# Layer 3's scans: where the additions over states run, who copies the exponents, and how many buffers they have

## The chip, the cores and the metric

The kernel runs on one core of a Trainium2 chip. A core has five engines that each work through their own list of instructions in order: PE (TensorE, matmul), DVE (VectorE), ACT (ScalarE), POOL (GpSimd) and SP (SyncE), which here mostly issues DMAs. They wait for each other by semaphores. The metric is the time of the whole kernel in microseconds on the device, the median over runs.

## The reference

Four layers are applied to x of shape (4, 96, 56, 56), each as x + layer(group norm of x): attention, a selective scan over eight directions, a windowed top-k aggregation, and a second kind of scan over four directions. Only the last one's scan is touched. For each direction k, batch b, channel d (192) and position t (3136), with 16 states n:

```python
dA  = dlt[..., None] * A_log[None, :, :, None, :]
phi = jnp.exp(-jnp.cumsum(dA, axis=3))
dbx = dlt[..., None] * jnp.swapaxes(b, 2, 3)[:, :, None] * xs[..., None]
h   = phi * jnp.cumsum(dbx / (phi + 1e-12), axis=3)
y   = jnp.einsum('bkdln,bknl->bkdl', h, c) + Ds[None, :, :, None]
```

So phi is the exponential of a running sum, the input is divided by phi (plus a tiny number), summed up along t, and multiplied by phi again; the last line adds up the 16 states with weights c.

## The kernel before, in words

`cumulative` does this. The positions are cut into chunks of 93 and a chunk into three blocks of 31. Two directions (one forward, one backward) go side by side, so a chunk has six blocks, taken in pairs; there are 34 chunks for each of two pairs of directions: 68 chunks, 408 blocks. In a block, partition 32b+t is batch b and position t (31 positions and one row for the carry), and the free dimension has 6 groups of channels x 16 states x 32 channels = 3072 elements.

What is done for one block, with the lines of the profile:

- `zhalf(st, h)`, twice: PE multiplies the running sums of delta by A for eight of the states (L1297) into a PSUM tile `z` that has one buffer. ScalarE copies it (L1305, 1536 elements) into its half of the tile `phi`, which at first holds exponents. The first half also allocates `phi`, from a pool with five buffers.
- `inverse(st)`: ScalarE's sigmoid of phi gives 1/(exp + tiny) into `w` (L1313, three buffers). `phis(st)`: ScalarE turns phi into exponentials in place (L1321). Each has its table load (1283 ns).
- `weights(st)`: PE brings delta times u into a PSUM tile `misc` (L1329); GpSimd builds the matrix `m` from C, the triangle and B (L1336 to L1338, three buffers).
- `into_sum(st)`: VectorE multiplies w by that tile in place (L1345); then SP loads the carry of this direction, 48 KB, from the DRAM tensor `l3cr` into four rows of w (L1346).
- `sums(st, q)`, q = 0 to 3: PE multiplies m by w for four states each (L1357) into a PSUM tile `q` with two buffers.
- `times(st, q)`: VectorE multiplies phi by that in place, 768 elements (L1366).
- `carry(st)`: SP stores four rows of phi to `l3cr` (L1370). The block after next, which is of the same direction, loads them in its L1346.
- `out(st)`: the sum over the 16 states. VectorE adds the halves of phi into a tile `t` (L1376, 1536 elements) and the halves of that (L1377, 768); GpSimd adds 384 elements (L1378) and 192 into `y` (L1380, two buffers); SP stores y with four DMAs (L1388).

`prepare` makes a chunk's inputs, the chunk before being at work. It is a generator; `tick` runs it to its next `yield`, twice for each block. Its pieces are loads of u, small matmuls with copies on ScalarE, two softplus (the "wide" step, L1186 and L1191 to L1193, which use the tile z), loads of C (L1199), du on GpSimd (L1228), and for each direction VectorE's L1233, a scan of 752 elements (L1241) and L1243.

The order is written out by hand. `in_order` chains the instructions of each engine, SP's DMAs among them, in the order in which the program calls them; nothing is rescheduled. The loop at the end of `cumulative` works on the pair `now`, prepares the pair `nxt` and starts the exponents of `third`. For one block st, with `coming_up` the next: inverse or phis of a later block, weights(coming_up), times 0 and 1, sums 2 and 3, zhalf(third, 0), inverse or phis of another, into_sum(coming_up), times 2 and 3, carry(st), tick, zhalf(third, 1), sums 0 and 1 of coming_up, tick, out(st). If the tick was the wide one, zhalf(third, 1) comes after the two sums.

Of the kernel before, what the change touches and what calls it, by code (L numbers as in the profile page):

```python
# [9 lines left out]
F32 = mybir.dt.float32  # L10
AF = mybir.ActivationFunctionType
ALU = mybir.AluOpType
# [9 lines left out]
DI, NS, R = 192, 16, 6  # L22
# [9 lines left out]
def view(ap, offset, dims):  # L32

    return bass.AP(ap.tensor, ap.offset + offset, [ap.ap[0], *dims])
# [35 lines left out]
class Net:  # L70
# [1027 lines left out]
    def cumulative(self, us, dram):  # L1098


        nc, tc = self.nc, self.tc
# [6 lines left out]
        with in_order(tc), ExitStack() as cx:  # L1108
# [179 lines left out]
            def zhalf(st, h):  # L1288
                s, i = st["s"], st["i"]
                lo = TW - TB * (i + 1) if s["rev"] else TB * i  # L1290
                st["lo"] = lo
                z = psz.tile([128, 3, 2, 8, 32], F32, name="z")
                for dh in range(2):
                    for b in range(B):
                        for p in range(3):
                            ps_ = slice(32 * p, 32 * p + 32)
                            nc.tensor.matmul(  # L1297
                                z[32 * b : 32 * b + 32, p, dh].rearrange("p n d -> p (n d)"),
                                s["s"][ps_, dh, b, lo : lo + 32],
                                st["ad"][ps_, dh, 8 * h : 8 * h + 8, :].rearrange("p n d -> p (n d)"),  # L1300
                                start=True, stop=True,
                            )
                if h == 0:
                    st["phi"] = big.tile([128, 3, 2, NS, 32], F32, name="phi", bufs=5)
                nc.scalar.copy(  # L1305
                    st["phi"][:, :, :, 8 * h : 8 * h + 8, :].rearrange("p a b n d -> p a b (n d)"),
                    z.rearrange("p a b n d -> p a b (n d)"),
                )
# [63 lines left out]
            def out(st):  # L1372
                s, i, lo, k = st["s"], st["i"], st["lo"], st["k"]
                phi = st["phi"].rearrange("p a b n d -> p (a b) (n d)")
                t = p2.tile([128, 6, 8 * 32], F32, name="t", bufs=1)
                nc.vector.tensor_tensor(t, phi[:, :, 0:256], phi[:, :, 256:512], ALU.add)  # L1376
                nc.vector.tensor_tensor(t[:, :, 0:128], t[:, :, 0:128], t[:, :, 128:256], ALU.add)  # L1377
                nc.gpsimd.tensor_tensor(t[:, :, 0:64], t[:, :, 0:64], t[:, :, 64:128], ALU.add)  # L1378
                y = p2.tile([128, DI], F32, name="y")
                nc.gpsimd.tensor_tensor(  # L1380
                    view(y, 0, [[32, 3], [96, 2], [1, 32]]),
                    view(t, 0, [[512, 3], [256, 2], [1, 32]]), view(t, 32, [[512, 3], [256, 2], [1, 32]]),
                    ALU.add,
                )
                a, e = max(lo, s["off"]), min(lo + TB, s["off"] + s["tv"])
                at = s["t0"] + a - s["off"]
                for b in range(B):
                    nc.sync.dma_start(  # L1388
                        ys[k][b, at : at + e - a, :], y[32 * b + a - lo : 32 * b + e - lo, :]
                    )  # L1390
# [5 lines left out]
            def draw():  # L1396
                return [next(todo, None) for _ in range(2)]

            now, nxt = draw(), draw()
            for st in (*now, *nxt):  # L1400
                zhalf(st, 0)
# [9 lines left out]
            while now[0] is not None:  # L1411
                third = draw()
                for i, st in enumerate(now):
                    coming_up = (now[1], nxt[0])[i]
                    what = (inverse, phis)[i]
                    if nxt[0] is not None:
                        what(nxt[0])
                    if coming_up is not None:
                        weights(coming_up)
                    times(st, 0)  # L1420
                    times(st, 1)
                    sums(st, 2)
                    sums(st, 3)
                    if third[i] is not None:
                        zhalf(third[i], 0)
                    if nxt[1] is not None:
                        what(nxt[1])
                    if coming_up is not None:
                        into_sum(coming_up)
                    times(st, 2)  # L1430
                    times(st, 3)
                    carry(st)
                    wide = tick()[1]
                    if third[i] is not None and not wide:
                        zhalf(third[i], 1)
                    if coming_up is not None:
                        sums(coming_up, 0)
                        sums(coming_up, 1)
                    if third[i] is not None and wide:
                        zhalf(third[i], 1)  # L1440
                    tick()
                    out(st)
                now, nxt = nxt, third
        return ys

    def layer3(self, xin, xout, dram):
# [284 lines left out]
```

## Time and profile before

| | us |
|---|---|
| three runs, median | 16579.15 |
| lowest and highest | 16575.54, 16581.78 |
| the profiled execution | 16544.92 |
| its span | 16543.1 |
| first to last L1366 (layer 3's scans) | 10927.2 to 15715.9 |
| mean granted clock of TensorE | 0.911 |

Busy over the whole span: PE 13366.7 us (81%), DVE 13918.8 (84%), ACT 12240.4 (74%), POOL 7665.0 (46%). These are averages over four layers with different limits; for this change the stretch in the table's fifth row counts. A row of the groups reads: line, engine, operation, output<-inputs, shapes, how often, then busy time and mean duration in ns, then the idle time of that engine just ahead of it and what ended it. A row of the timeline is start, length, engine, line, operation, and in brackets the idle time ahead of it and its releaser. "SPq" is SP's queue of DMA issues, and its length is the time for issuing, not for the transfer.

### The profile page before, as it was taken

What the parts mean: (1) busy time and instruction counts of PE and PEld (TensorE: products, weight loads), DVE (VectorE), ACT (ScalarE), POOL (GpSimd) and SP (SyncE); (2) the same over time, 40 slices, a digit from 0 to 9 for tenths busy, and PEclk for the clock granted to TensorE, in tenths of its full rate; (3) what the DMA queues carried; (4) which work ended last, traced back from release to release, by engine and by line L of the source; (5) the groups of instructions that cost most, each with busy time, mean ns of one, the idle gap of its engine ahead of it and who ended that gap; (6) DMA issues with size and microseconds to landing.
All of it is one profiled execution on the core that took longest, in us unless ns stands there. A gap on an engine that the chain in (4) does not pass through costs nothing.

```text
span 16543.1 us, 501276 instructions
## 1 busy us (share of the span) xinstructions
PE 13366.7 (81%) x221976; PEld 8983.6 (54%) x221976; DVE 13918.8 (84%) x15345; ACT 12240.4 (74%) x15452; POOL 7665.0 (46%) x3968
## 2 busy tenths in 40 slices
PE   8999977777777777777776678778888888888866
PEld 4333325666666666666665445446666656666533
DVE  7666549999999999999998777768888888888866
ACT  0465449999999999999996244468888888888822
POOL 0000028888888888888885000023333333333300
PEclk6899889999999999999998588889999999999977
DMA  0000034334444434344445800122212222221122
GB/s 15 1 1 1 16 137 97 91 92 95 105 105 103 103 91 96 92 96 102 103 105 139 194 10 10 43 71 51 50 47 50 50 50 51 51 50 47 43 66 66
DMA packets 821402, 1152.50 MB, mean 70 GB/s; under 512 B 309360, under 2 KB 728720, under 8 KB 807456
## 3 DMA queue, kind: packets, MB, share of 16 engines
q1 hardware_dynamic: 759872, 1055.38, 26.3%
q10 hardware_dynamic: 53984, 45.77, 1.2%
q8 instruction: 1745, 28.59, 0.8%
q0 software_dynamic: 5376, 19.27, 0.4%
q14 instruction: 425, 3.48, 0.1%
HBM read 842.93 MB, written 277.18 MB: 68 GB/s over the span
## 4 chain that ended last, share of the span: by engine, by line
PE 32%; DVE 28%; ACT 19%; issue 15%; DMA 5%; SPq 1%; POOL 1%; DVEq 0%; ACTq 0%; POOLq 0%
DVE q L638 17%; PE q L1357 7%; ACT ht L663 5%; PE s L233 4%; ACT e L626 3%; PE d L417 3%; ACT phi L1305 3%; DVE w L1345 3%; PE z L1297 2%; PE acc L251 2%; PE m L196 2%; ACT w L1313 2%; PE t L561 2%; PE y L675 2%; DVE phi L1366 2%
## 5 line engine op out<-in xcount | busy, mean ns | idle before, releaser
L618 POOL TENSOR_TENSOR q<-du,bm 128x1792 f32<-128x1792 f32 x1344 | 5345.3, 4024 | 3.1 <-DMA bm<-bc 3.1
L638 DVE TENSOR_TENSOR_SCAN q<-e,state,q 128x448 f32<-128x448 f32 x4608 | 4874.1, 1122 | 142.7 <-ACT e L626 140.1
L626 ACT ACTIVATE e<-dl,na 128x448 f32<-128x448 f32 x5376 | 3355.4, 640 | 179.4 <-DVE q L638 123.7
L675 PE MATMUL y<-ht,cd 128*32 128x64 f32 x75264 | 1836.6, 225 | 1480.0 <-ACT ht L663 1479.5
L654 PE MATMUL t<-ident,q 128*128 128x128 f32 x18816 | 2611.9, 292 | 93.9 <-issue 77.8
L1357 PE MATMUL q<-w,m 32*32 32x192 f32 x52224 | 2573.2, 348 | 124.1 <-DVE phi L1366 71.2
L654 PEld LDWEIGHTS t<-ident,q 128*128 128x128 f32 x18816 | 2377.1, 203 | 324.4 <-issue 201.1
L663 ACT COPY ht<-t 128x896 f32<-128x896 f32 x2688 | 2428.3, 903 | 87.1 <-PE t L654 57.1
L675 PEld LDWEIGHTS y<-ht,cd 128*32 128x32 f32 x75264 | 1399.7, 110 | 1958.2 <-ACT ht L663 1942.9
L1357 PEld LDWEIGHTS q<-w,m 32*32 32x32 f32 x52224 | 1873.3, 113 | 737.7 <-issue 184.3
L1366 DVE TENSOR_TENSOR phi<-q,phi 128x768 f32<-128x768 f32 x1632 | 1512.4, 952 | 519.4 <-PE q L1357 491.7
L1378 POOL TENSOR_TENSOR t<-t 128x384 f32<-128x384 f32 x408 | 407.3, 998 | 2974.2 <-DVE t L1377 2974.2
L1297 PE MATMUL z<-ad,sm 32*32 32x256 f32 x39168 | 1277.4, 391 | 396.2 <-ACT phi L1305 382.0
L241 ACT ACTIVATE e<-s 128x896 f32<-128x896 f32 (+1 forms) x1050 | 921.7, 915 | 902.6 <-PE m L196 508.2
L1305 ACT COPY phi<-z 128x1536 f32<-128x1536 f32 x816 | 1164.5, 1427 | 526.5 <-PE z L1297 526.3
L208 DVE TENSOR_REDUCE pm<-m 128x1 f32<-128x448 f32 (+1 forms) x1672 | 982.9, 616 | 667.1 <-PE m L196 599.6
L1345 DVE TENSOR_TENSOR w<-w,misc 128x3072 f32<-128x3072 f32 x408 | 1364.8, 3345 | 82.7 <-PE misc L1329 47.0
L1313 ACT ACTIVATE w<-phi,lntiny,w_k_rmask 128x3072 f32<-128x3072 f32 x408 | 1203.1, 2949 | 2.6
L196 PE MATMUL m<-ka,qa 32*128 32x448 f32 (+1 forms) x3344 | 1169.3, 638 | 7.5 <-DVE pm L208 7.5
L1321 ACT ACTIVATE phi<-phi,w_k_nmask 128x3072 f32<-128x3072 f32 x408 | 1165.5, 2857 | 2.4
L1297 PEld LDWEIGHTS z<-ad,sm 32*32 32x32 f32 x39168 | 708.7, 104 | 659.6 <-ACT phi L1305 463.0
L292 POOL DMA_DIRECT2D x<-xc x28 | 14.5, 517 | 2178.4 <-DVE xc L291 2177.5
(255 smaller groups left out, 18928.9 us busy)
## 6 DMA issues: line engine op xcount, KB each, us to landing
bm<-bc SPq DMA_DIRECT2D x896, 448.0 KB
cm<-cd SPq DMA_DIRECT2D x544, 186.0 KB
l1y<-out SPq DMA_DIRECT2D x672, 96.0 KB
l1y<-out SPq DMA_DIRECT2D x672, 72.0 KB
y<-l1y ACTq DMA_DIRECT2D x224, 168.0 KB
l3y<-y SPq DMA_DIRECT2D x1616, 23.2 KB
w<-l3cr SPq DMA_DIRECT2D x408, 48.0 KB
l3cr<-phi SPq DMA_DIRECT2D x408, 48.0 KB
```

The costliest lines, as they stand in the source:

```text
L618: nc.gpsimd.tensor_tensor(q, spread(s["du"][:, j, :], ng), s["bm"][g], ALU.mult)
L626: nc.scalar.activation(e[:, :CH], s["dl"][:, j, :], AF.Exp, scale=na[:, s["k"], j, n : n + 1])
L638: nc.vector.tensor_tensor_scan(a, e, a, first, ALU.mult, ALU.add)
L654: nc.tensor.transpose(flat(t)[:, 128 * c : 128 * c + 128], view(q, h * NC2 + c, [[NC, 128]]), self.ident,)
L663: nc.scalar.copy(t, flat(s["t", j, g, h])[:, : NC2 * 128])
L675: nc.tensor.matmul(s["y", j][r : r + 32, c // 4, 64 * half : 64 * half + 64], s["cd"][:, half, g, c, :], s["t", j, g, h][:, 128 * i + 64 * ...
L1297: nc.tensor.matmul(z[32 * b : 32 * b + 32, p, dh].rearrange("p n d -> p (n d)"), s["s"][ps_, dh, b, lo : lo + 32], st["ad"][ps_, dh, 8 * h ...
L1305: nc.scalar.copy(st["phi"][:, :, :, 8 * h : 8 * h + 8, :].rearrange("p a b n d -> p a b (n d)"), z.rearrange("p a b n d -> p a b (n d)"),)
L1313: nc.scalar.activation(w.rearrange("p a n d -> p (a n d)"), st["phi"].rearrange("p a b n d -> p (a b n d)"), AF.Sigmoid, bias=lntiny, scal ...
L1345: nc.vector.tensor_tensor(st["w"], st["w"], ut, ALU.mult)
L1357: nc.tensor.matmul(qp[bs, n, :DI], st["m"][bs, 4 * q + n, :], st["w"][bs, :, 4 * q + n, :], start=True, stop=True,)
L1366: nc.vector.tensor_tensor(ph, view(st[q], 0, [[256, 4], [32, 6], [1, 32]]), ph, ALU.mult)
```

## The change

Four things in `cumulative`, nothing else:

- the additions over states are all GpSimd's, and work in phi itself: three additions in place (1536, 768 and 384 elements), and the last one of 192 reads phi instead of t. The tile t is gone.
- `out` of a block is called one block later: `summed` holds the block, and `out(summed.pop())` comes in the next block's turn behind weights(coming_up) and ahead of its times 0; the last block's comes after the loop.
- the copy of the second half of the exponents is VectorE's.
- phi has six buffers.

```diff
                 if h == 0:
-                    st["phi"] = big.tile([128, 3, 2, NS, 32], F32, name="phi", bufs=5)
-                nc.scalar.copy(
+                    st["phi"] = big.tile([128, 3, 2, NS, 32], F32, name="phi", bufs=6)
+                (nc.scalar.copy if h == 0 else nc.vector.tensor_copy)(
...
                 phi = st["phi"].rearrange("p a b n d -> p (a b) (n d)")
-                t = p2.tile([128, 6, 8 * 32], F32, name="t", bufs=1)
-                nc.vector.tensor_tensor(t, phi[:, :, 0:256], phi[:, :, 256:512], ALU.add)
-                nc.vector.tensor_tensor(t[:, :, 0:128], t[:, :, 0:128], t[:, :, 128:256], ALU.add)
-                nc.gpsimd.tensor_tensor(t[:, :, 0:64], t[:, :, 0:64], t[:, :, 64:128], ALU.add)
+                for half in (256, 128, 64):
+                    nc.gpsimd.tensor_tensor(
+                        phi[:, :, 0:half], phi[:, :, 0:half], phi[:, :, half : 2 * half], ALU.add
+                    )
                 y = p2.tile([128, DI], F32, name="y")
                 nc.gpsimd.tensor_tensor(
                     view(y, 0, [[32, 3], [96, 2], [1, 32]]),
-                    view(t, 0, [[512, 3], [256, 2], [1, 32]]), view(t, 32, [[512, 3], [256, 2], [1, 32]]),
-                    ALU.add,
+                    view(st["phi"], 0, [[1024, 3], [512, 2], [1, 32]]),
+                    view(st["phi"], 32, [[1024, 3], [512, 2], [1, 32]]), ALU.add,
                 )
...
+            summed = []
             now, nxt = draw(), draw()
...
                     if coming_up is not None:
                         weights(coming_up)
+                    if summed:
+                        out(summed.pop())
                     times(st, 0)
...
                     tick()
-                    out(st)
+                    summed.append(st)
                 now, nxt = nxt, third
+            out(summed.pop())
```

## The prediction

> **What bounds the kernel now.** I read the busy times of the stretch in which layer 3's scans run, then its groups of instructions, then the timeline of one plain block, then who waits on SP's queue. The stretch goes from the first to the last L1366, 10927.2 to 15715.9 us: 4788.7 us for 408 blocks, 11.74 each, 70.4 for a chunk of six. All of the change lies in it. First the windows of one chunk (columns: window, length, busy PE, PEld, DVE, ACT, POOL, granted clock, DMA share, GB/s):
>
> ```profile
> 14015.00:14035.40 20.40, 20.38 (x536) 14.08 (x520) 19.55 (x16) 19.93 (x14) 7.63 (x10) 1.00 0.09 23
> 14035.40:14049.60 14.20, 12.23 (x242) 7.85 (x248) 9.63 (x8) 11.32 (x10) 5.53 (x6) 0.88 0.52 126
> ```
>
> The first row is two plain blocks: PE, VectorE and ScalarE are all full, GpSimd is 37% busy. That alone invites moving work to GpSimd. The second row is the block with the softplus of the next chunk ("wide"): nobody is full. Groups of the stretch, from 12000 to 15000 us:
>
> ```profile
> L1345 DVE TENSOR_TENSOR w<-w,misc 128x3072 f32<-128x3072 f32 x256 | 856.4, 3345 | 31.0 <-PE misc L1329 31.0
> L1305 ACT COPY phi<-z 128x1536 f32<-128x1536 f32 x511 | 729.1, 1427 | 317.8 <-PE z L1297 317.8
> L1376 DVE TENSOR_TENSOR t<-phi 128x1536 f32<-128x1536 f32 x256 | 449.2, 1755 | 20.5 <-DVE phi L1366 3.7
> L1337 POOL TENSOR_TENSOR m<-cm,w_k_tri 128x496 f32<-128x496 f32 x255 | 296.5, 1163 | 0.0
> L1338 POOL TENSOR_TENSOR m<-m,bt 128x512 f32<-128x512 f32 x255 | 267.2, 1048 | 20.0
> L1378 POOL TENSOR_TENSOR t<-t 128x384 f32<-128x384 f32 x255 | 254.6, 998 | 1836.3 <-DVE t L1377 1836.3
> L1377 DVE TENSOR_TENSOR t<-t 128x768 f32<-128x768 f32 x255 | 244.2, 958 | 8.8
> L1380 POOL TENSOR_TENSOR y<-t 128x192 f32<-128x192 f32 x255 | 150.4, 590 | 20.0
> ```
>
> And the path through one plain block, lines of the timeline (start, length):
>
> ```profile
> 13007.78 0.48 SPq L1346 DMA_DIRECT2D w<-l3cr  x1
> 13009.51 0.50 SPq L1370 DMA_DIRECT2D l3cr<-phi  x1
> 13010.85 2.80 PE L1357 MATMUL q<-w,m 32*32 32x192 f32 x64 [0.17 <-DMA w<-l3cr]
> 13012.47 0.96 DVE L1366 TENSOR_TENSOR phi<-q,phi 128x768 f32<-128x768 f32 x1 [0.17 <-PE q L1357]
> 13013.72 0.96 DVE L1366 TENSOR_TENSOR phi<-q,phi 128x768 f32<-128x768 f32 x1 [0.29 <-PE q L1357]
> 13014.08 1.42 SPq L1388 DMA_DIRECT2D l3y<-y  x4
> 13014.59 3.34 DVE L1345 TENSOR_TENSOR w<-w,misc 128x3072 f32<-128x3072 f32 x1
> 13017.96 0.50 SPq L1346 DMA_DIRECT2D w<-l3cr  x1
> ```
>
> A full VectorE is not the whole of it. The load of the carry into w (L1346) starts at 13007.78, lands 2.94 later (the chain of waits has it as one piece), PE begins the sums 0.13 after that, VectorE's first product 1.62 later, the second 1.25 after it, into_sum 0.87 after it, and 3.37 later the next L1346 starts: 2.94+0.13+1.62+1.25+0.87+3.37 = 10.18. So a plain block is a closed loop load, sums, two products, into_sum, load; VectorE's tree (L1376, L1377) runs while the load and the first sums do. Removing it doesn't shorten the loop. Last, SP's own waits from 12000 to 15000 us (total, times, longest):
>
> ```profile
> SPq L1388 <- POOL y L1380: 671.4, 235, 5.9
> ```
>
> SP stands still for y before it stores it, 2.86 us each time. It now costs nothing, because what stands behind it, L1346, waits for into_sum anyway.
>
> **The change, part by part.**
>
> *VectorE's tree goes.* 1.755+0.958 = 2.71 us per block off VectorE. On the loop: nothing, by the sum above. The two scan blocks of a chunk take 13.09 and 11.45, there a scan (1.72, with 0.17 and 0.16 around it) is added to VectorE's queue, and some could come back.
>
> *The second copy of exponents goes to VectorE.* 1.43 off ScalarE. On VectorE no such copy exists; its copies out of PSUM take 541 ns for 384 elements (L688) and 273 for 128 (L689), so 1.05 ns per further element: 541+1152x1.047 = 1.75 us. Bounds from other PSUM rows: 1.67 (L1345's rate) and 1.90 (L1366's). VectorE's balance is -0.96 us. Queued behind this copy are the next block's products. In a plain block PE's second half of z ends 3.2 after into_sum (13021.13 against 13017.93), the copy ends at 5.0, the products start at 4.6 at the earliest: 0.4 lost every second block at most, taken as nothing while the load is later still (below). In the wide block PE does z after both sums, so the copy holds up products that were already fed: there 1.75 plus the wait count.
>
> *The tree goes to GpSimd.* Two adds are new, 1536 and 768 elements; those of 384 and 192 stay. From 192 (590 ns) to 384 (998) an element costs 2.125 ns over 182 fixed: 182+3264 = 3.45 and 182+1632 = 1.81. This line gives 3.99 for 1792 elements, and the row L618 has 4.02. So out takes 3.45+1.81+1.00+0.59 and three gaps of 0.08 = 7.09 (it was 1.67). Bounds by the cheapest and dearest rate, L1338's 2.05 and L1378's 2.60 per element: 6.5 and 7.8. GpSimd then has 7.1+2.4 (L1336 to L1338) per block and 1.79 for du twice a chunk, 9.5 to 11.3: it isn't the bound by throughput.
>
> GpSimd runs beside VectorE. The Trainium skill, "GPSIMD Engine Reference", section 8, says that the two share SBUF interfaces and contend when a VectorE instruction has two SBUF inputs. L618 runs beside VectorE's scans of layer 1 and stands 1% above the line through the two small adds; by the trace this adds 0.05 us, and the rule gives no figure.
>
> *In place, one block later.* Three things become ordered. (a) The first add overwrites phi, whose rows the carry's store (L1370) reads: GpSimd must wait for it to land. No row shows that landing. The nearest rows are the load of the same 48 KB on the same queue, 2.94, and a store of 168 KB, out<-o, whose median to landing is 2.4; I take the middle, 2.70. Bounds are 2.4 and 4.19, a load of 672 KB (u<-l1u1rows in the chain of waits). (b) y comes 7.09 after that, and then its four stores, 1.40 of SP's issue. (c) In block j's turn `out` of j-1 is called ahead of into_sum of j+1, so these stores now stand on SP's queue ahead of the carry's load (L1346) for j+1. SP works in order, as its waits show. So a new loop closes, from one L1346 to the next: its issue 0.50, the carry's store behind it 2.70, 0.13 until GpSimd starts, 7.09, 0.03, 1.40 of stores = 11.85. That is longer than 10.18. When L1346 did not wait, the carry's data come 1.85 after into_sum instead of 0.50: 13.20.
>
> *The sixth buffer.* phi lives one block longer and has one buffer more: ScalarE's copy into it needs out of six blocks earlier, which ended half a block before. Nothing. The one out after the loop adds about 7 at the end.
>
> **The sum.** The chunk from 14003.77 has L1346 intervals of 11.55, 10.02, 10.01, 14.28 (wide), 13.09 and 11.45 (scans), 70.40. After:
> - after the second scan block the load is 1.0 late (13.2 against the 12.2 of VectorE's chain below), so the carry's data come 1.85-1.0 = 0.85 after it instead of 0.50: 12.2 for the first plain block; then 11.85 and 11.85.
> - wide: the load is 11.85-10.18 = 1.7 late, so PE's softplus matmuls (done 4.72 after into_sum) no longer hold up the sums: they start at 3.1, z ends 5.65 later as before, copy 1.75, two products 1.82, into_sum 3.35: 15.7.
> - first scan: z ends at 4.56, copy 1.75, scan 2.05, products 1.82, into_sum 3.3: 13.5; the SP loop gives 13.2.
> - second scan: the SP loop, 13.2 (z's copy ends at 4.85, scan 2.05, products 1.82, into_sum 3.35 and 0.1 of starts make 12.2).
>
> Together 78.3, +7.9. For 67 chunks 529; the last blocks and the last out +15: +544. The profiled execution took 16544.9, so 17089; the median of the three runs is 34 above it, so about 17120.
>
> **The clock.** PE's granted clock was 0.69 between 14039 and 14043, after an idle stretch of 1.97 us ahead of L1186 and its narrow matmuls. With a longer block PE idles more: about 1.4 and 2.0 us in two pieces. If each block's sums run at the slow row (4.54 for the 64 matmuls that take 2.80 above) the load's slack of 1.7 hides it; through z and its copy the worst I find is 2.97+0.13+4.54+0.54+4.3+2.3+1.44+0.25+2.3+1.75+5.25 = 25.8 for two blocks, 12.9. The Trainium skill, "TensorE: Matmul & The Clock Gate", part 1, has half clock only after an idle window of about 3.4 us; the trace lost it sooner. By the rule these pieces cost nothing; by the trace 0 to 1.05 a block.
>
> **Rivals.**
> 1. *The SP loop doesn't close* (store lands early, adds fast): for L1346 not to wait, landing plus out must fit into 10.18-1.85-0.16-1.40 = 6.8 us. Only the copies ahead of the products remain: wide 17.2, scans 13.6 and 12.2, plain 10.2: 73.7, +3.3, +220: 16800. Against: the cheapest rows give 2.4+6.5 = 8.9.
> 2. *Faster: VectorE was the bound after all.* Its 0.96 per block comes off, 6x67x0.96 = 386: 16190. For: 19.55 of 20.40. Against: the loop of 10.18 holds no instruction that goes. It decides only if y is stored before into_sum ends, the same 6.8 us.
> 3. *Same*: the queue hides everything but the wide copies, and the scan blocks give that back: 16580.
> 4. *PE goes slow in each block*: 12.9 in place of 11.85 in four of six, +1.05x4x67 = 281: 17400.
>
> **Chances.** Forecast 0.66, first rival 0.11, second 0.09, third 0.03, fourth 0.11. What a measurement of this kernel can tell from no change is 0.2%. Faster 0.09, same 0.03, slower 0.88. The landing at 4.19 adds 1.49 to four blocks and 1.2 to the first scan, 480: 17600; out at 7.8 adds 0.7, some 210: 17330; out at 6.5 and landing at 2.4 together take 0.9 from four, 240: 16880. The range reaches from the first rival, 16790, to 17600.
>
> **What would show it.** Right: SP's wait for y at about 6 to 9 us a block and the wait of L1346 gone behind it; PE waiting for DMA w<-l3cr, or VectorE for PE q, 1.7 us a block more; the first add on GpSimd waiting for the store of l3cr; adds at 3.4 and 1.8; VectorE near 75% and ScalarE near 72% busy; plain blocks at 11.9. Wrong: L1346 still 0.03 after into_sum, plain blocks at 10.2 or below. The forecast falls if the stores of y don't hold up L1346, and shrinks with every tenth that the landing is shorter.

## The result, and the profile after

The changed kernel takes 18072.6 us (median of four runs, 18066.85 to 18075.37); the kernel before took 16577.35 beside it. That is 1.091 times as long, interval 1.0894 to 1.0925. The forecast was 17120, with a range up to 17600: the sign was right, the size was not, 950 us too low. The profiled execution has a span of 18073.6 and a mean granted clock of 0.880 (before 0.911).

All of it lies in layer 3's scans. The mean chunk of six blocks takes 93.2 us instead of 70.5. By the medians of the six intervals between issues of L1346 (first scan, second scan, three plain, wide):

| us | scan | scan | plain | plain | plain | wide |
|---|---|---|---|---|---|---|
| before | 13.02 | 11.45 | 11.59 | 10.09 | 10.10 | 14.16 |
| forecast | 13.5 | 13.2 | 12.2 | 11.85 | 11.85 | 15.7 |
| after | 16.22 | 16.29 | 13.19 | 14.63 | 13.66 | 18.68 |

So every kind of block is slower than forecast: the scans by 5.8 together, the plain ones by 5.6, the wide one by 3.0.

First the groups of the changed kernel from 12000 to 15000 us:

```profile
L1376 POOL TENSOR_TENSOR phi<-phi 128x1536 f32<-128x1536 f32 x193 | 664.9, 3445 | 977.2 <-DMA l3cr<-phi 887.9 <-ACT x L1170 28.5 <-DVE phi L1305 23.9
L1376 POOL TENSOR_TENSOR phi<-phi 128x768 f32<-128x768 f32 x194 | 447.7, 2308 | 15.2
L1305 DVE COPY phi<-z 128x1536 f32<-128x1536 f32 x193 | 339.3, 1758 | 734.1 <-issue 265.4 <-POOL phi L1376 219.3 <-PE z L1297 188.0
L1233 DVE TENSOR_TENSOR dl<-dl,tot 96x8 f32<-96x8 f32 x62 | 129.3, 2085 | 0.0
L1243 DVE COPY tot<-sm 96x8 f32<-96x8 f32 x64 | 102.2, 1597 | 2.2
```

The two costs that the prediction worked out from other shapes are there: 3.45 for the 1536 additions, 1.76 for the copy. But two instructions of 8 elements, L1233 and L1243, now take 2.085 and 1.597 on average, and the 768 addition has a mean of 2.31 where 1.81 was worked out. The same two in the kernel before:

```profile
L1243 DVE COPY tot<-sm 96x8 f32<-96x8 f32 x86 | 14.4, 168 | 2.9
L1233 DVE TENSOR_TENSOR dl<-dl,tot 96x8 f32<-96x8 f32 x84 | 13.4, 159 | 0.0
```

Next SP's queue, its waits in the same stretch:

```profile
SPq L1388 <- POOL y L1380: 1299.2, 161, 10.7
SPq L1346 <- DVE w L1345: 255.7, 126, 5.7
```

The first stood at 671.4 before. The second was this line before:

```profile
SPq L1346 <- DVE w L1345: 787.6, 256, 12.3
```

SP waits for into_sum in 126 of 194 blocks and 1.3 us a block on average, where it was 3.1 before: in part of the blocks it now comes to the load when into_sum is done already. There the loop over SP that was forecast is closed; in the others it is not, though the forecast had this wait gone. With the wait that the profile puts down to L1145 on GpSimd (330.5), SP stands 8.4 us a block ahead of y's stores; 6 to 9 had been forecast.

Now two plain blocks of the changed kernel, lines of the timeline (start, length):

```profile
13027.43 1.41 SPq L1388 DMA_DIRECT2D l3y<-y  x4
13028.95 0.50 SPq L1346 DMA_DIRECT2D w<-l3cr  x1
13029.55 0.50 SPq L1370 DMA_DIRECT2D l3cr<-phi  x1
13033.95 5.03 PE L1357 MATMUL q<-w,m 32*32 32x192 f32 x64 [3.88 <-DMA w<-l3cr]
13034.45 6.41 POOL L1376 TENSOR_TENSOR phi<-phi 128x1536 f32<-128x1536 f32 x3 [4.74 <-DMA l3cr<-phi]
13036.87 0.96 DVE L1366 TENSOR_TENSOR phi<-q,phi 128x768 f32<-128x768 f32 x1 [4.94 <-PE q L1357]
13039.05 0.96 DVE L1366 TENSOR_TENSOR phi<-q,phi 128x768 f32<-128x768 f32 x1 [1.23 <-PE q L1357]
13039.93 3.34 DVE L1345 TENSOR_TENSOR w<-w,misc 128x3072 f32<-128x3072 f32 x1
13041.55 1.41 SPq L1388 DMA_DIRECT2D l3y<-y  x4
13043.30 0.50 SPq L1346 DMA_DIRECT2D w<-l3cr  x1
13045.03 0.50 SPq L1370 DMA_DIRECT2D l3cr<-phi  x1
13048.08 2.80 PE L1357 MATMUL q<-w,m 32*32 32x192 f32 x64 [1.64 <-DMA w<-l3cr]
13048.58 6.44 POOL L1376 TENSOR_TENSOR phi<-phi 128x1536 f32<-128x1536 f32 x3 [4.76 <-DMA l3cr<-phi]
13055.72 1.40 SPq L1388 DMA_DIRECT2D l3y<-y  x4
13057.23 0.50 SPq L1346 DMA_DIRECT2D w<-l3cr  x1
```

The first block goes round the old loop, with worse terms. From load to load: the load lands and PE starts 5.00 after its issue (2.94+0.13 = 3.07 before), the first product 2.92 later (1.62), the second 2.18 after it (1.25), into_sum 0.88 (0.87), the next load 3.37 (3.37): 14.35. The second block goes round the loop over SP: the carry's store 1.73 after the load, the first addition 3.55 after that, y's stores 7.14 after the addition, the next load 1.51 after them: 13.93. Additions and stores are as forecast (7.09 and 1.40). The transfers are not. With the 0.13 until the next engine starts, the load takes 5.00 and 4.78 where 3.07 had been taken, the store 4.90 and 3.55 where 2.83 had been taken. In the second block the load did not have to wait for y's stores, and for this case the prediction had 13.20; the store's 0.7 more makes it 13.9. The first block stands outside the forecast: there the old loop is the longer one again.

And PE's granted clock while it works off the two pairs of sums (columns as in the windows shown before):

```profile
13033.95:13038.90 4.95, 4.95 (x64) 3.34 (x64) 0.96 (x1) 2.12 (x1) 4.37 (x2) 0.54 0.02 4
13048.10:13050.90 2.80, 2.80 (x68) 2.35 (x72) 1.16 (x2) 2.77 (x4) 2.32 (x1) 1.00 0.04 9
```

After 3.88 us without work the clock is 0.54 and the same 64 matmuls take 5.03; after 1.64 us it is 1.00 and they take 2.80. From 12000 to 15000 us the second plain block of a chunk has its first sums below 0.75 (mean of the 2.5 us from their start) in 31 of 33 chunks, none of 43 before; the third in 9 of 32, none of 42 before. So the prediction's fourth rival came true in one plain block of a chunk and at times in a second, at 2.2 us where 1.05 had been put down. It is not so everywhere: the first plain block has the low clock in 2 of 32 chunks where it had it in 25 of 43 before, and the wide block has it in all, as it did before. Its sums there, before and after:

```profile
13044.95 5.00 PE L1357 MATMUL q<-w,m 32*32 32x192 f32 x57
```

```profile
13063.33 4.97 PE L1357 MATMUL q<-w,m 32*32 32x192 f32 x57 [3.33 <-DMA w<-l3cr]
```

Last, a second scan block. The additions of GpSimd one by one, and VectorE beside them:

```profile
13003.97 3.44 POOL L1376 TENSOR_TENSOR phi<-phi 128x1536 f32<-128x1536 f32 x1 [4.16 <-DMA l3cr<-phi]
13006.81 0.63 DVE L1233 TENSOR_TENSOR dl<-dl,tot 96x8 f32<-96x8 f32 x1
13007.48 1.72 DVE L1241 TENSOR_TENSOR_SCAN sm<-starts,dl 96x752 f32<-96x752 f32 x1
13007.49 3.32 POOL L1376 TENSOR_TENSOR phi<-phi 128x768 f32<-128x768 f32 x1
13009.24 1.60 DVE L1243 COPY tot<-sm 96x8 f32<-96x8 f32 x1
13010.75 1.81 DVE L1366 TENSOR_TENSOR phi<-q,phi 128x768 f32<-128x768 f32 x2
```

L1233 has 8 elements and ends at 13007.44, when the 1536 addition does (13007.41). The scan L1241 then runs at its usual 1.72, and the 768 addition, started beside it, takes 3.32 instead of 1.81. L1243, again 8 elements, ends at 13010.84, with that addition (13010.81). Each stands still until the other's instruction is through; they take turns. This is no single case: in the changed kernel 267 of the 268 instructions L1233 and L1243 take over 0.3 us, and each of the 267 ends within 0.06 us of the end of an instruction of GpSimd. VectorE's products wait behind it.

### The profile page after: what moved, and what is told of

Read it like the earlier page. It is cut to its first block, busy times and chain, and to the rows that moved or that the text cites. A ratio compares the mean times of both kernels' runs of the same rounds, so it can differ in the third digit from the quotient of the medians.

```text
span 18073.6 us, 501814 instructions
## 1 busy us (share of the span) xinstructions
PE 13774.3 (76%) x221976; PEld 9184.6 (51%) x221976; DVE 13955.1 (77%) x14937; ACT 11716.1 (65%) x15044; POOL 10006.3 (55%) x4784
## 5 line engine op out<-in xcount | busy, mean ns | idle before, releaser
L618 POOL TENSOR_TENSOR q<-du,bm 128x1792 f32<-128x1792 f32 x1344 | 5348.2, 4024 | 3.6 <-DMA bm<-bc 3.3
L1357 PE MATMUL q<-w,m 32*32 32x192 f32 x52224 | 2969.7, 384 | 1337.8 <-DVE phi L1366 798.4
L1376 POOL TENSOR_TENSOR phi<-phi 128x1536 f32<-128x1536 f32 (+2 forms) x1224 | 2752.4, 2249 | 2164.7 <-DMA l3cr<-phi 1910.4
L1357 PEld LDWEIGHTS q<-w,m 32*32 32x32 f32 x52224 | 2079.6, 125 | 2127.1 <-issue 855.3
L1305 ACT COPY phi<-z 128x1536 f32<-128x1536 f32 x408 | 586.9, 1438 | 2589.6 <-issue 1388.7
L1305 DVE COPY phi<-z 128x1536 f32<-128x1536 f32 x408 | 717.2, 1758 | 1545.2 <-issue 553.4
```

Of the source, the lines that this page charges most:

```text
L618: nc.gpsimd.tensor_tensor(q, spread(s["du"][:, j, :], ng), s["bm"][g], ALU.mult)
L1305: (nc.scalar.copy if h == 0 else nc.vector.tensor_copy)(st["phi"][:, :, :, 8 * h : 8 * h + 8, :].rearrange("p a b n d -> p a b (n d)"), z. ...
L1357: nc.tensor.matmul(qp[bs, n, :DI], st["m"][bs, 4 * q + n, :], st["w"][bs, :, 4 * q + n, :], start=True, stop=True,)
L1376: nc.gpsimd.tensor_tensor(phi[:, :, 0:half], phi[:, :, 0:half], phi[:, :, half : 2 * half], ALU.add)
```

## The experiments

The reasons to be told apart: the loop over SP (theory of the prediction), late landings, the slow clock, the taking of turns between VectorE and GpSimd, and the copy ahead of the products. Every run was compared with runs of the kernel before on the same chip (medians 16558 to 16569; 16577 for the change itself). The last column is six times the mean interval of L1346 over the whole stretch (before 70.5); where the load is in two pieces, the first counts.

| run | median us | ratio to before | chunk us |
|---|---|---|---|
| the change | 18072.6 | 1.0910 [1.0894, 1.0925] | 93.2 |
| e1_stores_later | 17464.01 | 1.0545 [1.0529, 1.0561] | 84.2 |
| e2_later_small | 17048.27 | 1.0298 [1.0278, 1.0318] | 78.0 |
| e3_copy_back | 17641.62 | 1.0653 [1.0637, 1.0669] | 86.5 |
| e4_first_add_dve | 17947.86 | 1.0838 [1.0820, 1.0856] | 90.9 |
| e5_tree_alone | 16488.16 | 0.9951 [0.9934, 0.9969] | 69.8 |
| e6_into_sum_ahead | 17632.31 | 1.0642 [1.0626, 1.0658] | 86.8 |
| e7_ahead_second_add | 17533.97 | 1.0583 [1.0565, 1.0600] | 85.2 |
| e8_copy_alone | 18216.97 | 1.0996 [1.0980, 1.1013] | 95.2 |
| e9_du_ahead | 16434.86 | 0.9914 [0.9899, 0.9929] | 68.7 |
| e10_halves | 16423.04 | 0.9909 [0.9894, 0.9923] | 68.5 |
| e11_long_adds | 16504.99 | 0.9959 [0.9945, 0.9973] | 70.0 |
| e12_later_alone | 16555.75 | 0.9993 [0.9983, 1.0002] | 70.8 |
| e13_stores_between | 18706.01 | 1.1300 [1.1284, 1.1317] | 102.4 |
| e14_two_loads | 16613.41 | 1.0036 [1.0023, 1.0049] | 71.7 |
| e15_stores_behind | 16534.80 | 0.9985 [0.9976, 0.9995] | 70.6 |

### e1_stores_later: y's stores behind the carry's store

The changed kernel, with y's four stores issued at the end of the turn:

```diff
+                return k, y, lo, a, e, at
+
+            def store(k, y, lo, a, e, at):
                 for b in range(B):
...
-                    if summed:
-                        out(summed.pop())
+                    made = out(summed.pop()) if summed else None
...
                     tick()
+                    if made is not None:
+                        store(*made)
```

> The changed kernel (18072.6 us, 93.2 us a chunk of six), but SP issues the four stores of y at the end of the turn, behind the carry's store, instead of ahead of the carry's load (L1346). Theory Q (the loop on SP's queue: load, carry's store, GpSimd's four additions, y's stores, next load, with both transfers lengthened because y's stores lie just ahead of them): the load goes out 0.03 us after into_sum in every block and lands in 2.9 instead of 4.8 to 5.0, PE's sums are never at the slow clock in plain blocks, and plain blocks fall from 13.1 to 14.7 us to 10.2 to 10.5. The two scan blocks keep what VectorE's small instructions lose beside GpSimd (15 to 16 us), the wide one about 17: some 79 us a chunk, 17100 us. Rival G (GpSimd's 7.1 us of additions or PE's clock set the pace by themselves): plain blocks stay above 13, 18000 us. Rival B (VectorE was the bound before, and only the queue hides the gain): below 16400.

It takes 609 us off the change. Two lines of the waits of this kernel, 12000 to 15000 us:

```profile
SPq L1346 <- DVE w L1345: 1611.0, 214, 13.5
PE q L1357 <- DMA w<-l3cr: 0.4, 2, 0.2
```

SP waits for into_sum again and PE hardly ever for the load, on which it starts some 3.0 after the issue. Plain blocks are back at 10.04, the first of a chunk at 11.49, as before. But scan blocks stay at 14.8 and 17.6 and the wide one at 18.5. So y's stores ahead of the load, with SP's wait for y, the late landing and the clock that is lost by it, are some 600 of the 1500, and something else has the rest.

### e2_later_small: and the additions cut into pieces

```diff
-                    nc.gpsimd.tensor_tensor(
-                        phi[:, :, 0:half], phi[:, :, 0:half], phi[:, :, half : 2 * half], ALU.add
-                    )
+                    n = 6 if half == 64 else 2
+                    for g in range(0, 6, n):
+                        nc.gpsimd.tensor_tensor(
+                            phi[:, g : g + n, 0:half], phi[:, g : g + n, 0:half],
+                            phi[:, g : g + n, half : 2 * half], ALU.add
+                        )
```

> As the first run, and GpSimd's additions of 1536 and of 768 elements are cut into three pieces each (512 and 256 elements), about 1.0 us more of GpSimd a block. Theory X (a VectorE instruction with two SBUF inputs, or a copy from SBUF to SBUF, waits until GpSimd's running instruction has ended): L1233, 1.90 us in the median after the change, falls to at most 1.3 and 0.6 in the mean, L1243 from 1.60 to at most 1.3; scan blocks are 1.5 to 2.5 us shorter than in the first run, the total 200 to 330 us shorter. If the two merely share bandwidth for the length of the additions, L1233 and L1243 keep their lengths and the total stays within 100 us of the first run or above.

Another 416 us come off, more than expected. Cutting adds work to GpSimd (0.18 us for each further instruction, by the fixed part of the prediction's line) and yet helps: a short instruction of VectorE now waits for a third of an addition. L1233's mean goes from 1957 ns in e1 to 447, L1243's from 2033 to 1038, the second scan block from 17.6 to 15.8, the first from 14.8 to 12.7 and the wide one from 18.5 to 17.0. So the taking of turns is a cost of its own here.

### e3_copy_back and e8_copy_alone: the copy by itself

e3 is the changed kernel with both copies on ScalarE; e8 the kernel before with only this edit:

```diff
-                nc.scalar.copy(
+                (nc.scalar.copy if h == 0 else nc.vector.tensor_copy)(
```

> The changed kernel with ScalarE doing both copies of the exponents again. Theory Q plus C (the copy on VectorE stands ahead of the next products and costs its 1.75 us in the wide and the scan blocks): plain blocks keep 13 to 14.7 us, wide and scan blocks lose 1 to 2 us each, 4 us a chunk, 270 us: about 17800. If the copy is what made the kernel slow: below 17000. If it hides everywhere: within 40 us of 18070.

> The kernel before with one part of the change: VectorE does the second copy of the exponents. VectorE then has 11.6 us a plain block and becomes its bound: with copy and tree both in front of the next products, plain blocks stand at 11.6 to 12 instead of 10.1, wide and scan blocks are 2 to 3 us longer; 11 us a chunk, 750 us: about 17300. If the copy hides behind VectorE's waits: below 16750.

Both show more than was expected: undoing the copy takes 431 us off the change, and the copy alone costs 1659, more than the whole change. In e8 no addition has moved, L1233 and L1243 stand at 159 and 168 ns, and y's stores go out well ahead of the load. Its timeline, VectorE, PE and ScalarE:

```profile
13005.19 1.44 ACT L1305 COPY phi<-z 128x1536 f32<-128x1536 f32 x1 [4.22 <-PE z L1297]
13007.09 1.36 PE L1297 MATMUL z<-ad,sm 32*32 32x256 f32 x48
13008.50 1.76 DVE L1305 COPY phi<-z 128x1536 f32<-128x1536 f32 x1 [1.50 <-PE z L1297]
13010.17 1.75 DVE L1376 TENSOR_TENSOR t<-phi 128x1536 f32<-128x1536 f32 x1
13011.95 0.96 DVE L1377 TENSOR_TENSOR t<-t 128x768 f32<-128x768 f32 x1
13012.83 1.81 DVE L1366 TENSOR_TENSOR phi<-q,phi 128x768 f32<-128x768 f32 x2
13013.83 3.88 PE L1357 MATMUL q<-w,m 32*32 32x192 f32 x57 [2.06 <-DVE phi L1366]
```

That is a closed loop, from the products at 13000.18 to those at 13012.83: products, the sums 2 and 3 that need their PSUM tiles, the first half of z behind these on PE, ScalarE's copy, a few small matmuls of `prepare` on PE, the second half of z in the same tile, VectorE's copy, and behind it in VectorE's own order the tree and the next products. 12.65 long, and PE, which idles in it, comes to run below full clock (3.88 for 57 matmuls that took 2.62 a block earlier). Before, ScalarE made that copy, and the products did not stand behind it. In the changed kernel the tree is out of this loop; that would explain why the copy costs less there, but no run tests it by itself.

### e5_tree_alone, e11_long_adds, e12_later_alone: the change without the copy

e5 is e2 with ScalarE's copies; e11 the same with the additions whole (that is e1 with ScalarE's copies); e12 the kernel before with `out` one block later and nothing else, phi with five buffers:

```diff
+                    if summed:
+                        out(summed.pop())
                     times(st, 0)
...
-                    out(st)
+                    summed.append(st)
```

> The second run's kernel (y's stores behind the carry's store, short additions; 17048 us, 77.3 us a chunk) with ScalarE doing both copies again: of the change only GpSimd's tree, one block later and in place, is left. Theory C (VectorE's copy stands ahead of the next products): wide blocks come down from 16.8 to 18.5 us to about 14 to 15, scan blocks by about 1.5, some 6 us a chunk, 400 us: about 16650, within 1% of the kernel before. If GpSimd's additions cost by themselves, over VectorE's small instructions or by their length: above 16850. If taking the tree off VectorE is worth what it was taken for (2.7 us a block): below 16300.

> The fifth run's kernel with the additions of 1536 and 768 elements in one piece each, as the change has them: the price of their length alone, without VectorE's copy and with y's stores out of the way. Theory X: L1233 and L1243 take 1.6 to 3 us again, the scan blocks are 1.5 to 2.5 us longer each, 16750 us. If it was the copy that put these instructions beside the additions: 16490 within 50, or less, as GpSimd has 1.0 us a block less to do.

> The kernel before with one part of the change: out is called one block later (tree on VectorE and GpSimd into t as before, five buffers). Nothing on VectorE's or SP's queue changes its place by it, only GpSimd's two additions come behind weights: within 0.3% of the kernel before by each theory of mine. If the later call itself is a cost (phi's buffers held longer, y's stores nearer to the load): 16800 or more, with plain blocks above 10.5.

e12 shows that the later call alone is worth nothing either way. e5 and e11 are 0.5% and 0.4% faster than before, with no difference between them that counts. Two things follow. First, with the tree gone from VectorE the second and third plain block still take 10.03 and 10.06 (10.09 and 10.10 before), although VectorE is far from full. Those two of one chunk of e5:

```profile
13000.88:13021.18 20.30, 20.28 (x524) 14.00 (x520) 13.81 (x11) 20.10 (x14) 19.75 (x24) 1.00 0.10 25
```

That the loop of 10.18 is the reason is not shown by this. ScalarE is busy for 20.10 of the 20.30 us, and for 19.93 of 20.40 in the row that the prediction shows from before: its own work holds these blocks where they are as well as the loop does (e10 comes back to it). The small gain is mostly in the first plain block, the one behind the scans: 11.28 us on average before, 10.30 in e5 and 10.71 in e11.

Second, whole additions cost no more than 0.1% against cut ones here, within the intervals, where they cost 416 us with the copy in place. L1233 and L1243 stand at 604 and 501 ns in e11, against 1957 and 2033 in e1; 136 of the 268 take over 0.3 us there, 234 in e1. So the taking of turns is dear only in company: with the copy, VectorE's order puts more of the scan's small instructions beside the long additions.

The effects do not add up. From the change, the stores' order is worth 609 and the copy 431; both together (e11) are worth 1568.

### e4_first_add_dve: the longest addition on VectorE

```diff
-                    nc.gpsimd.tensor_tensor(
+                    (nc.vector if half == 256 else nc.gpsimd).tensor_tensor(
```

> The changed kernel with the first addition (1536 elements) on VectorE again, in place in phi; GpSimd keeps those of 768, 384 and 192, 3.6 us instead of 7.1. Theory Q: the SP loop is 3.5 us shorter; with the transfers at their undisturbed lengths 0.50+2.6+0.13+3.6+0.03+1.40 = 8.3, so it no longer holds the load up, and plain blocks are 10.2 to 11. Scan blocks lose less beside GpSimd (its longest instruction is 1.8 instead of 3.4). Some 75 us a chunk, 16850 us. Rival G with PE's clock as the cause: plain blocks stay near 13.

A miss by 1100 us, and a useful one. Without the addition of 1536, `out` on GpSimd takes 3.6 us and L1233 and L1243 are back at 159 and 168 ns, but the time hardly falls. Part of it, I think, is that VectorE now has copy and addition ahead of its products (wide blocks 21.3). Another part is in its timeline:

```profile
13062.49 3.34 DVE L1345 TENSOR_TENSOR w<-w,misc 128x3072 f32<-128x3072 f32 x1
13064.57 1.41 SPq L1388 DMA_DIRECT2D l3y<-y  x4
13066.09 0.50 SPq L1346 DMA_DIRECT2D w<-l3cr  x1
13071.11 4.26 PE L1357 MATMUL q<-w,m 32*32 32x192 f32 x64 [2.10 <-DMA w<-l3cr]
```

The load is issued as soon as into_sum has ended (0.26 us after it here), so SP's wait for y no longer delays its issue. But it stands right behind y's stores, and PE starts 5.02 after it.

### e13_stores_between, e14_two_loads, e15_stores_behind: stores ahead of a load, by themselves

Three kernels from the one before, to measure that by itself. y's stores are kept back until the next into_sum; the carry's load is cut into two halves of two rows. e13 has the stores between the halves, e14 ahead of both:

```diff
                 nc.sync.dma_start(
-                    st["w"][31:128:32].rearrange("p a n d -> p (a n d)"), crs[st["k"]]
+                    st["w"][31:64:32].rearrange("p a n d -> p (a n d)"), crs[st["k"]][0:2]
+                )
+                store()
+                nc.sync.dma_start(
+                    st["w"][95:128:32].rearrange("p a n d -> p (a n d)"), crs[st["k"]][2:4]
                 )
```

e15 has the load whole and `store()` behind it.

> The kernel before, with the carry's load cut in two DMAs of two rows each, and between them, on the same queue, the four stores of y of the block before last (y is ready by then, so SP waits for nothing but into_sum). Theory (a transfer issued right behind y's four stores lands late, 4.8 to 5.0 instead of 2.94): PE starts about 0.50+1.40+4.9 = 6.8 after the first half's issue instead of 2.94+0.13, so a plain block takes about 13.9 and the chunk grows by some 3.7 x 5 = 18: about 17800. Rival (the stores cost only their issue, and the late landing in the changed kernel came from something else): PE starts 1.9 later, plain blocks near 12.1, chunk +9, about 17200.

> The control: the same two halves of the load, one right behind the other, and y's four stores ahead of both, issued as soon as SP reaches them, while it would otherwise wait for into_sum. Both theories: the second half is issued 0.5 to 0.6 later, so PE starts 0.55 later than before at most; plain blocks 10.2 to 10.7, the chunk +0 to +3, 16560 to 16770.

> The load in one piece as before, and y's four stores directly behind it, ahead of the carry's store. If only what stands ahead on the queue delays a transfer: the load lands after 2.9, plain blocks 10.0 to 10.2, about 16570, while the carry's store is issued 1.9 or more after the load and lands late (some 4.9 instead of 2.7), which nobody waits for. If what stands behind delays it as well: PE starts 1 to 2 later, plain blocks 11 to 12, 16900 to 17300.

The timeline of e13 (L1350 is the second half), and that of e14, where the two halves are L1347 and L1350:

```profile
13001.84 1.65 SPq L1397 DMA_DIRECT2D l3y<-y  x4
13003.53 0.48 SPq L1350 DMA_DIRECT2D w<-l3cr  x1
13008.58 5.13 PE L1361 MATMUL q<-w,m 32*32 32x192 f32 x60 [3.89 <-DMA w<-l3cr]
```

```profile
13010.97 1.35 SPq L1397 DMA_DIRECT2D l3y<-y  x4
13014.25 0.48 SPq L1347 DMA_DIRECT2D w<-l3cr  x1
13014.78 0.46 SPq L1350 DMA_DIRECT2D w<-l3cr  x1
13017.43 4.65 PE L1361 MATMUL q<-w,m 32*32 32x192 f32 x64 [0.47 <-DMA w<-l3cr]
```

From the second half's issue to PE's start it is 5.05 with the stores directly ahead and 2.65 without; over the whole run, where PE waited for the load, the medians are 5.08 and 2.64. e13 takes 13% longer than before, the control 0.4%. It is beyond even the theory's 17800; the theory left out the clock, and all 176 first pairs of sums between 12000 and 15000 us run below 0.75. e15 settles the other direction: with the stores behind the load PE starts 2.94 after its issue (median), and the time is that of before. So the 2 us in the changed kernel come from the stores ahead, and they need neither late additions nor a waiting SP.

The other kernels have the same at greater distances. Sorted by the time from the end of the stores' issue to the load's, PE starts this long after the load's issue (medians over its waits for the load; groups of more than ten waits, and one far row):

| stores' end to load, us | kernel, waits | load to PE, us | sum, us |
|---|---|---|---|
| 0.11 | changed, 142 | 5.04 | 5.15 |
| 0.64 | changed, 43 | 4.49 | 5.14 |
| 1.32 | e4, 13 | 3.75 | 5.11 |
| 1.59 | e4, 43 | 3.44 | 5.03 |
| 1.90 | before, 61 | 3.15 | 5.05 |
| 3.47 | changed, 5 | 3.04 | 6.52 |

Up to 1.9 us the sum stays the same: the load does not take a fixed 2 us more. In these rows PE starts on it some 5.0 to 5.2 us after the stores' issue has ended, whenever the load itself is issued.

### e6_into_sum_ahead and e7_ahead_second_add: a way round the loop that failed

e6 tried to shorten the plain block's loop in the kernel before, by weights one turn earlier and into_sum at the head of the turn (with the call of `draw()`, which can run the rest of `prepare`, behind it); e7 adds the 768 addition on GpSimd and y's stores a turn later:

```diff
                     if coming_up is not None:
-                        weights(coming_up)
+                        into_sum(coming_up)
...
-                    if coming_up is not None:
-                        into_sum(coming_up)
                     times(st, 2)
...
+                    if nxt[i] is not None:
+                        weights(nxt[i])
```

> The kernel before, with one thing reordered: weights of a block are called one turn earlier and into_sum at the head of the turn, ahead of the products, so that the carry's load has most of a turn to land. Theory L (a plain block of 10.1 us is a loop of load, sums, two products and into_sum, and VectorE's 9.87 us only just fit into it): plain blocks lose the loop and stand at VectorE's or ScalarE's work, 9.9 to 10.1, no more than 0.2 us less; blocks with scans, 11.45 to 13.1, stay within 1 us. Some 69 us a chunk, 16450 us. If the loop alone were the bound and the engines had slack: below 16000. If the order of before was needed for something else: above 16700.

> The fifth expectation's reordering (into_sum at the head of the turn) on the kernel before, and the second addition (768 elements) moved from VectorE to GpSimd, into the tile t as before; y's stores are issued one turn later, behind the carry's store. VectorE has 8.9 us a block, ScalarE 9.9, GpSimd 6.4. Theory L: with the loop gone VectorE's relief counts, but ScalarE is next: plain blocks 9.9, scan blocks 11 to 12; some 68 us a chunk, 16400 us, below the run with the order alone by up to 100 us. If GpSimd beside VectorE costs by itself, as in the scan blocks of the change: above that run.

Both are misses, 6% slower than before. A line of e6's waits shows one that is new:

```profile
DVE w L1345 <- PE misc L1329: 533.3, 171, 6.9
```

into_sum now stands ahead of the products on VectorE and waits for delta times u, which PE makes behind the matmuls for z. Before, this wait came to 31.0 us. I read no more than that from these two.

### e9_du_ahead and e10_halves: what beats both kernels

e9 is e5 with `out` called at the end of the turn, behind both ticks, so that du (L1228) goes ahead of the additions on GpSimd, and the stores a turn later still. e10 is e9 with into_sum in two halves, each with its half of the carry's load:

```diff
-                    if summed:
-                        out(summed.pop())
                     times(st, 0)
...
+                    if made:
+                        store(*made.pop())
+                    if summed:
+                        made.append(out(summed.pop()))
                     summed.append(st)
```

> The fifth run's kernel (GpSimd's tree in short additions, y's stores behind the carry's store, both copies on ScalarE; 16488 us), with out called at the end of the turn behind both ticks, so that GpSimd makes du (L1228) ahead of the additions and not behind them. Theory X: in the second scan block VectorE's L1233 waits 1.89 us for du and then 1.16 us in its own length; both go, and the block falls from 12.4 to about 11.4 us; the others stay. Some 70 us less, 16420 us. If the wait for du lies beside the loop anyway: 16488 within 30.

> As the run before it, and into_sum is cut into two halves of eight states, each followed by the load of its half of the carry: the sums 0 and 1 need the first half alone. Theory L (a plain block is the loop load 2.94, sums 1.62, products 2.1, into_sum 3.34; in the fifth run 10.02 us with VectorE at 7.2 and ScalarE at 9.94): the loop is 1.6 us shorter, ScalarE becomes the bound, plain blocks 9.9 to 10.0; scan and wide blocks, where ScalarE has slack, lose up to 1.6 each. Some 4 us a chunk, 16150 us. If ScalarE or GpSimd (10.6 us with its short additions) already set the pace: no difference, or plain blocks at 10.6.

e9 came out nearly as expected (16435 for 16420): 0.9% faster than before, 9% faster than the change. VectorE's wait for du ahead of L1233 (38.3 us between 12000 and 15000 in e5) is gone. e10 should have opened the loop and brought 270 more; it gives 12, within the interval. The window of its three plain blocks in one chunk says why:

```profile
12456.02:12485.96 29.94, 28.05 (x763) 20.45 (x746) 20.89 (x19) 29.42 (x20) 29.23 (x34) 1.00 0.17 42
```

ScalarE, the fourth column of busy times, is at 29.42 of 29.94, and GpSimd with its cut additions, the fifth, at 29.23. Two copies (1.43 each), the two functions (2.95 and 2.86) and a table load (1.28; two blocks' calls of a function share one, so it is one a block) are 9.95 a block on ScalarE. It was so before: in the second and third plain blocks of the kernel before, ScalarE is busy for 10.02 of 10.10 us on average. The loop stood beside an engine that was as long. This also says what the copy on VectorE could have been for: ScalarE would have to lose work with the loop open. No run does both, so that this would pay is not shown.

## Why the prediction was right and wrong

- **"Removing it doesn't shorten the loop": right in the time**, as e5 and e11 show; that the loop was the reason is not shown, since ScalarE's 9.95 a block gives the same time, and e10, which was to open the loop, gained nothing that can be measured.
- **The durations worked out from other shapes: right.** 3.45 (3.445 measured) and 1.75 (1.758); `out` as a whole 7.09, measured 7.14 from the first addition to the first store. The fixed part and the slope from two small additions of the same engine carried to eight times the size.
- **The loop over SP: right in kind.** SP waits 8.4 us a block for y, and e1 opens the loop again. But it does not set every plain block, as the forecast had it: in the two that are shown it takes turns with the old loop. One remark in (c) was loose: the stores did not move on the queue relative to the load, they had stood ahead of it before; y became late, and so they came to be issued directly ahead of it.
- **"I take the middle, 2.70", and 2.94 for the load: the terms that failed first.** Both were read where nothing stood directly ahead on the queue, as in the timeline of before, where the load comes 2.5 us after the last of y's stores. The loop that was forecast itself pushes the four stores against the load. Until the engine that waits for it starts, a load there takes 5.0, the store behind it 3.6 to 4.9. The bound of 4.19 was kept for the range, but for the store only; the load was taken to be undisturbed, and no row was asked what a transfer takes in its new place. e13 against e14 shows 2.4 us for this alone.
- **"the load's slack of 1.7 hides it": failed.** With the load at 5.0 there is no slack; PE idles for 3.9 us and then takes 5.03 for a pair of sums, 2.2 more, in the second plain block of nearly every chunk. The rival of the slow clock had 1.05 a block. In the changed kernel, from 12000 to 15000 us, all 101 idle stretches of over 3 us ahead of sums, with full clock until then, are followed by a clock below 0.75 (mean of 1.5 us), 28 of the 55 from 1.5 to 2.5 us as well, and none of the 20 from 1.0 to 1.5. The Trainium skill, "TensorE: Matmul & The Clock Gate", Part 1, has half clock after an idle window of about 3.4 us. That agrees with the longest of these stretches, but shorter ones lost the clock too, as did the 1.97 ahead of L1186 in the trace of before (0.69), and no run settled why.
- **"by the trace this adds 0.05 us": the second step that failed.** The comparison that it rested on, L618 beside VectorE's scans in layer 1, is not one: those scans read e, which lies in PSUM, so they have one input in SBUF. L1233 and L1241 have two, and L1243 copies from SBUF to SBUF. The Trainium skill, "SBUF — State Buffer", section "SBUF: two separate sides", describes the port pair that VectorE and GpSimd share as an exclusive lock for the whole instruction; the trace agrees, with 0.159 against 2.085 for L1233 and 3.32 against 1.81 for the 768 addition. The trace of before had it four times in 268, all at the start of layer 3's scans, where for one L1243 at 10876.25 took 3.34 beside a du of GpSimd; I had not looked at the longest of a group whose mean is 0.168. e2 puts 416 us on it, with stores and copy as they are there.
- **"taken as nothing while the load is later still": failed.** Undoing the copy is worth 431 us in the change (e3), and 959 once the stores are out of the way (e11 against e1). I priced it as one instruction ahead of the products. It also ties z's second half, PE's sums and VectorE's order into a loop (e8), and puts the small scan instructions beside the additions.
- **The wide block:** 15.7 had sums 3.1 after the load, 5.65 to z's end and 6.9 from there. In the block from 13057.23 it is 6.10, 6.95 and 6.77. The medians of the first two, from 12000 to 15000 us, are 6.14 and 5.83; before, the second was 5.64. So it is the load's landing alone that was missed, 3.0 of the 3.0 us; the slow clock was there before, and the copy is as forecast. Why the load takes 6.1 here and 5.0 in the plain blocks is open.

How the excess of 15 us a chunk divides between landing, clock and taking of turns is not settled: each makes the next worse, and no run took away one of them alone from the changed kernel and left the others as they were.

## What to carry to other kernels

When a change makes something late on an in-order queue, ask again what every transfer behind it will cost in its new place: a duration read where the queue was empty holds only there. An engine's balance of busy time says nothing for an instruction moved onto it until you have written down what then stands behind it in that engine's order, and whether this closes a loop. Before moving long work to GpSimd, look for VectorE's instructions that take their inputs from SBUF, and look at the longest one of each group, not at the mean.

## What the runs showed of the hardware

- PE starts on a 48 KB load 2.9 to 3.1 us after its issue, and 5.0 after it when four stores of 23 KB each, issued in 1.4 to 1.65 us, stand directly ahead of it on the same queue; with a load of half the size it is 5.05 instead of 2.65. With 0.1 to 1.9 us between the stores and the load, PE starts 5.0 to 5.2 after the end of the stores' issue. The same stores directly behind it change nothing (2.94).
- An instruction of 8 elements on VectorE can take as long as what is left of GpSimd's addition (up to 3.34 us measured; 267 of 268 in the changed kernel), and a scan on VectorE held up a GpSimd addition by 1.5 us.
- Cutting a long GpSimd addition into three, which adds work, made the kernel 416 us faster where 234 of 268 such instructions were held up (e1, e2), and made no measurable difference where it was 136 (e11, e5).
